# Moving a chunk's reciprocal ahead of the running sums, and work over the seam between two stages, in a fused attention and expert kernel

## The chip, the cores and the metric

The kernel runs on one core of a Trainium2 chip, in one launch. The metric is the device time of a launch in microseconds (us), the median of several runs. A core has five engines that run side by side, each with its own order of instructions: PE (TensorE, the matrix products; PEld are its weight loads), DVE (VectorE), ACT (ScalarE), POOL (GpSimd) and SP (SyncE, which here only issues DMAs). Matrix products write to PSUM, a memory of eight banks; a bank that is to be written again must first have been read by whoever needs its content. All times below are in us.

## The reference

The input `query` has 2048 tokens of 512 values. The output is the sum of the input, an attention and a layer of experts, both of the normalised input:

```python
x = L0_attn_query
xn = _layernorm(x, axis=-1)
x = x + attention(xn, Wq, Wk, Wv, Wout, ...) + experts(xn, gate_w, w1, w3, w2, sw1, sw3, sw2)
```

The attention has 16 heads, each with two causal softmaxes over the same values of width 32 (queries and keys are turned by rotary angles first). The two results are filtered along the sequence and subtracted, then each head is scaled to a root mean square of one and all heads go through Wout:

```python
f1 = jnp.fft.rfft(attn1, axis=1)
f2 = jnp.fft.rfft(attn2, axis=1)
attn_freq = (f1 - lambda_full * f2) * filt[None, :, None, None]
attn = jnp.fft.irfft(attn_freq, n=tgt_len, axis=1)
attn = attn * jax.lax.rsqrt(jnp.mean(attn * attn, axis=-1, keepdims=True) + EPS) * rms_weight
attn = attn * (1.0 - LAMBDA_INIT)
return attn.reshape(bsz, tgt_len, H * 2 * D) @ Wout
```

The experts are eight networks of hidden width 352, of which each token takes the two that a gate scores highest, and one shared network of hidden width 704 that every token takes. Each is `silu(x @ w1) * (x @ w3) @ w2`.

## The kernel before

**The stages.** From 0 to about 100 us the kernel loads the input, normalises and transposes it, makes the values and scores the gate, and sorts the tokens by expert. To about 253 it projects queries and keys, with the rotary turn, and does a part of the shared expert. From 253 to about 1252 runs `middle`: the attention's softmaxes with the experts threaded in. From there `ending` does the filter, the scaling by head, Wout and the final sums.

**The attention's order.** `middle` walks over 8 groups of two heads and, in each, over 4 chunks of 512 queries, from the last chunk to the first (`turns`). A chunk is cut into units, each with the keys of one or a few blocks; masked units, those on the diagonal, come last in a chunk. All units of all chunks stand in one list, `stream`, and the loop takes four of them per step. A step issues, in this order: the scores of two units (ps_s, L764, followed by ACT's exponentials to tiles pt, L777), the products of the previous step's pt with the values (ps_o, L804), the row sums of a chunk that has just ended (`sums`, ps_sum, L830), the scores of two more units, the rest of the products, on POOL the `put` of a chunk that was finished a step ago (L859), and then the part that the change touches:

- `added(before)` adds pt tiles to the running sums on DVE (L821; the first tile of a chunk is copied, L818). They were held back a step, because the sums' tiles were still in use.
- `added(...)` for the unmasked ones of the first two units of this step.
- `finish` (L837) of a chunk that ended a step ago: PE turns the chunk's output and row sums (ps_ot, four transposes, L842, and ps_st, one, L843); DVE takes the reciprocal of the row sums (rcp, L845), scales half of it (L848) and multiplies (o_n, L850).
- `work()` (L954), which takes the next piece of the experts' work, with `added` for the later units between the pieces, until the pace is met.
- `added` for the masked units, and on POOL a step or two of `folded` (L864; lines L870 to L912), the first part of the filter, for a group whose four chunks are through.

Each engine runs its own instructions in this order; nothing is reordered at run time.

**The experts' pieces.** `experts()` (L591) is a generator: each `next` issues a piece and gives back its estimated time. After the shared expert come 36 tiles of routed tokens. One tile takes an `up_first` (xh, L168, with ACT's tanh and DVE's L176), an `up_third` (xg, L168, with DVE's L182), a piece with the transposes of the next tile's tokens (ps_x, L159, and ACT's copy xT, L161) and the product of the tile before (`turned_back`, ps_u, L191, with DVE's copies uT, L193 and L194, and `down`, xy, L201, with ACT's result y_sb, stored by SP). The up weights come in wu, the down weights in wd, both fetched by SP two tiles ahead. The loop takes pieces until `worked / work_all` reaches the share of units done, with four units of lead (L999). `work_all` (L923) comes to 467.6 of the estimates' units.

**The banks.** In `middle` the scores take four PSUM banks, the values' product ps_o one, and a pool of three (fps, L577) serves everything else in turn: ps_sum, ps_ot, ps_st, and every tile of the experts (xh, xg, xy, ps_x, ps_u, wh, wy). A tile that is asked for while all three are held waits until the oldest has been read.

**The end of the attention.** After the loop, the last two chunks are closed one after the other (L1019 on): `sums`, `next(ex)`, `finish`, and `put`, here on DVE. Then the rest of the experts' pieces is issued, and the folds that are left, the last group's on DVE.

**The end stage.** `ending` (L1032) first asks for its tables on ACT's queue (conv, then the shared expert's last down weights, then wo_sb, the weights of Wout) and for the first twelve residual tiles (res: the input by SP's queue, then three sums into it by POOL's). The filter is a set of small products (ps_r and ps_z, L1082) with sums between them on DVE (L1127 on). It gives 16 tiles of 128 tokens, taken as eight `Pair`s: `prepared` makes y on DVE and squares it on ACT, `means` reduces and takes the root on ACT (L1162 on), `scales` refines the root and makes a (L1175) on DVE. A tile then goes `across` (L1198: ps_tr, four transposes on PE, and ACT's copy to aT, L1204), is `projected` (L1207: po, four products with wo_sb, L1210) and `finished` (L1213: DVE adds po to res, L1215, and SP's queue writes it out, L1216). `finished` also issues the loads of the four last res tiles.

Of the kernel before, what the change touches and what calls it, by code (L numbers as in the profile page):

```python
# [8 lines left out]
F32 = mybir.dt.float32  # L9
# [10 lines left out]
P = 128  # L20
T = 2048
E = 512
D = 16
NT = T // P
NE = E // P
# [37 lines left out]
def block_kernel(  # L63
# [7 lines left out]
    nc = tc.nc  # L71
# [206 lines left out]
    with ExitStack() as pools:  # L278
# [95 lines left out]
        for c in range(NE):  # L374
            for i in range(NQC):
                nc.tensor.matmul(
                    gt_ps[32 * i : 32 * i + 32, 0, :], gw_sb[:, c, :], xnT[:, c, i * QC : (i + 1) * QC],
                    start=(c == 0), stop=(c == NE - 1), skip_group_check=True,
# [41 lines left out]
        for t in range(NT):  # L420
# [5 lines left out]
                start=False, stop=(t == NT - 1), skip_group_check=True,  # L426
# [131 lines left out]
    def middle(general):  # L558


        with ExitStack() as pools:
# [358 lines left out]
            for n, turn in enumerate(turns):  # L920
                chunk = Chunk(*turn)
                stream += [(n, chunk, unit) for unit in chunk.units()]
            work_all = (NT - 1 - EARLY) * ((2 * SCH - 1) * 3.45 / TQ + 5.2) + NR * 8.5  # L923
            ex = experts()
            for c in range(NQC):
                load_keys(0, c)
# [43 lines left out]
            for i in range(0, len(stream), 4):  # L970
                units = stream[i : i + 4]
                found = burst(units[:2])
                n, ended = values()
                for c in closing:
                    c.sums()
                    summed += 1
                if n < 2 and not closing:

                    work()
                found += burst(units[2:])  # L980
                while todo:
                    ended += values()[1]
                todo += found
                for c in closed:
                    c.put(nc.gpsimd)
                    if c.qc == 0:
                        ready.append(c.g)
                closed, closing = closing, ended
                held, before = [], held
                added(before)  # L990
                added(u for u in units[:2] if not masked(u))
                later = [u for u in units[2:] if not masked(u)]
                for c in closed:
                    c.finish()
                while True:
                    work()
                    added(later[:1])
                    later = later[1:]
                    if worked / work_all >= (i + 4) / len(stream):  # L999
                        break  # L1000
                added(later)
                added(u for u in units if masked(u))
                if any(map(masked, units)) or not shared:
                    steps = 0
                else:
                    steps = 1 if len(ready) < 2 or any(map(masked, stream[i + 4 : i + 8])) else 2
                for _ in range(steps):
                    if folding is None and ready:
                        folding = folded(ready.pop(0), nc.gpsimd)
                    if folding is not None and next(folding, 0) == 0:  # L1010
                        folding = None
# [20 lines left out]
    def ending():  # L1032
# [3 lines left out]
        with tc.tile_pool(name="tail1", bufs=1) as t1, tc.tile_pool(name="tail", bufs=2) as tp, tc.tile_pool(  # L1036
# [161 lines left out]
            def across(k):  # L1198

                ptr = fps.tile([P, NE, P], F32, tag="f", name="ps_tr")  # L1200
                for c in range(NE):
                    nc.tensor.transpose(ptr[:, c, :], pairs[k // 2].a[:, k % 2, c * P : (c + 1) * P], ident)
                aT = tp.tile([P, NE, P], F32, tag="aT", name="aT")
                nc.scalar.copy(aT, ptr)  # L1204
                return aT

            def projected(aT):  # L1207
                po = fps.tile([P, E], F32, tag="f", name="po")
                for c in range(NE):
                    nc.tensor.matmul(po, aT[:, c, :], wo_sb[:, c, :], start=(c == 0), stop=(c == NE - 1))  # L1210
                return po

            def finished(k, po):  # L1213
                res = came[k]
                nc.vector.tensor_add(res, res, po)  # L1215
                nc.sync.dma_start(out_t[:, order[k], :], res)  # L1216
                for step in range(4):
                    if 12 <= k + 9 - step < NT:
                        fetched(k + 9 - step, step)
# [11 lines left out]
            pairs.append(prepared(1))  # L1231
            pairs[0].means()
            y = result(us, 0)
            nc.vector.tensor_sub(dv, z, dv)
            pairs[0].scales()
            aT = across(0)
            pairs[1].means()
            po = None
            for n in range(NT // 2):
                after = across(2 * n + 1)  # L1240
                ahead, po = po, projected(aT)
                if n + 1 < NT // 2:
                    pairs[n + 1].scales()
                if n == 0:
                    stored(y, ysh[NT - 1], 0.5)
                if n + 2 < NT // 2:
                    pairs.append(prepared(n + 2))
                if n + 1 < NT // 2:
                    aT = across(2 * n + 2)
                if ahead is not None:  # L1250
                    finished(2 * n - 1, ahead)
                if n + 2 < NT // 2:
                    pairs[n + 2].means()
                now, po = po, projected(after)
                finished(2 * n, now)
            finished(NT - 1, po)

    with tc.If(nc.values_load(more[0:1, 0:1], min_val=0, max_val=1) > 0):  # L1258

# [129 lines left out]
```

## Time and profile before

| | us |
|---|---|
| three runs | 1369.66, 1371.17, 1373.96 |
| median | 1371.17 |
| the profiled execution | 1372.31 |
| its span in the trace | 1370.5 |

The mean granted clock of TensorE was 0.992 of full speed. The costliest groups of instructions, weight loads left out (busy us in total, and mean ns of one):

| line and operation | count | busy us | mean ns |
|---|---|---|---|
| L821 DVE, running sums | 576 | 622.1 | 1130 |
| L777 ACT, exponentials | 544 | 527.8 | 1024 |
| L804 PE, product with the values | 2560 | 266.0 | 534 |
| L764 PE, scores | 1280 | 205.4 | 407 |
| L782 POOL, causal mask | 256 | 170.2 | 689 |
| L231 PE, shared expert, up | 352 | 151.2 | 578 |
| L520 PE, queries and keys | 256 | 110.5 | 593 |
| L201 PE, routed experts, down | 216 | 99.8 | 598 |
| L168 PE, routed experts, up (xh) | 288 | 96.9 | 482 |
| L168 PE, routed experts, up (xg) | 288 | 94.1 | 470 |

The prediction shows lines of several views. The **page** gives each engine's busy time and share, and the share of each engine in the **chain**, which is the work that ended last, followed back from the end. The **waits** list, for one engine, which instruction waited for what: total us, number of times, longest. The **timeline** gives instructions in order: start, duration, engine, line, operation, what it writes and reads, shape, count, and in square brackets the idle time before it with what ended it. The **stretches** give, for a window of time, the busy time of each engine in it, the granted clock of TensorE (1.00 is full), the share of the DMA engines' time and GB/s.

### The profile page before, as it was taken

How to read it: one execution, taken by the hardware profiler on the slowest of the kernel's cores; microseconds unless marked ns; L12 is line 12 of the kernel's file. 1: busy time of each engine (PE TensorE's matmuls, PEld its weight loads, DVE VectorE, ACT ScalarE, POOL GpSimd, SP SyncE). 2: the span in 40 equal slices, each digit the busy share in tenths (PEclk: the TensorE clock that was granted, in tenths of full speed). 3: DMA queues.
4: the chain of work that ended last, by engine and by line, in shares of the span. 5: the costliest groups of instructions: out<-in, count | busy, mean ns of one | idle time of the engine just before them, and what ended most of it. 6: DMA issues, size and time to landing. Idle time of an engine off the chain costs nothing.

```text
span 1370.5 us, 20621 instructions
## 1 busy us (share of the span) xinstructions
PE 1325.6 (97%) x7472; PEld 614.9 (45%) x7472; DVE 1005.0 (73%) x1337; ACT 690.6 (50%) x853; POOL 565.9 (41%) x673
## 2 busy tenths in 40 slices
PE   7999999999999999998999999999999999998998
PEld 3444444333443454444444444544444454444543
DVE  7048882378777867867787788798788878787785
ACT  2311110265655656665666566666666656662321
POOL 0001222111401232136964655576468437534863
PEclk9999999999999999999999999999999999999999
DMA  9405662201211122355655656656656565548996
GB/s 376 171 16 181 202 198 80 87 10 37 77 40 32 44 73 67 89 151 173 207 172 167 182 189 195 200 182 193 201 155 215 184 197 187 180 142 261 177 200 142
DMA packets 74689, 206.58 MB, mean 151 GB/s; under 512 B 12028, under 2 KB 12192, under 8 KB 69200
## 3 DMA queue, kind: packets, MB, share of 16 engines
q1 hardware_dynamic: 61840, 177.62, 40.4%
q0 software_dynamic: 11216, 23.31, 8.2%
q10 hardware_dynamic: 1520, 4.23, 0.9%
q8 instruction: 62, 1.02, 0.3%
q14 instruction: 51, 0.42, 0.1%
HBM read 161.26 MB, written 43.85 MB: 150 GB/s over the span
## 4 chain that ended last, share of the span: by engine, by line
PE 68%; DVE 8%; issue 2%; ACT 1%; DMA 1%; POOL 1%; DVEq 0%; ACTq 0%
PE ps_o L804 16%; PE ps_s L764 12%; PE wh L231 9%; PE xh L168 7%; PE xg L168 6%; PE xy L201 6%; PE wy L269 4%; DVE sum L821 3%; PE ps_sum L830 2%; PE po L1210 1%; DMA wd<-in_wex_dram 1%; PE ps_ot L842 1%; PE ps_u L191 1%; PE ps_z L1082 1%; PE ps_x L159 1%
## 5 line engine op out<-in xcount | busy, mean ns | idle before, releaser
L821 DVE TENSOR_TENSOR sum<-sum,pt 128x1024 f32<-128x1024 f32 (+2 forms) x576 | 622.1, 1130 | 32.2 <-ACT pt L777 16.2
L777 ACT ACTIVATE pt<-ps_s 128x1024 f32<-128x1024 f32 x544 | 527.8, 1024 | 177.3 <-PE ps_s L764 110.4
L782 POOL TENSOR_SCALAR_AFFINE_SELECT pt<-pt 128x256 f32<-128x256 f32 x256 | 170.2, 689 | 331.5 <-ACT pt L777 276.0
L804 PE MATMUL ps_o<-pt,vd 128*32 128x512 f32 (+3 forms) x2560 | 266.0, 534 | 1.3 <-POOL pt L782 1.3
L764 PE MATMUL ps_s<-qS,kS 64*128 64x512 f32 (+3 forms) x1280 | 205.4, 407 | 2.0 <-DVEq L1258 1.6
L764 PEld LDWEIGHTS ps_s<-qS,kS 64*128 64x128 f32 x1280 | 97.2, 185 | 173.3 <-issue 95.1
L231 PE MATMUL wh<-xnT,wu 128*128 128x512 f32 (+1 forms) x352 | 151.2, 578 | 0.0
L804 PEld LDWEIGHTS ps_o<-pt,vd 128*32 128x32 f32 x2560 | 66.7, 109 | 130.3 <-issue 116.0
L473 POOL DMA_INDIRECT who<-pairs,slot x32 | 34.2, 1069 | 202.5 <-DVE pairs L470 101.3
L859 POOL TENSOR_TENSOR vd<-o_n 128x128 f32<-128x128 f32 x60 | 43.3, 742 | 172.4 <-DVE o_n L850 149.9
L520 PE MATMUL ps_x<-xnT,wqk_sb 128*128 128x512 f32 x256 | 110.5, 593 | 0.0
L201 PE MATMUL xy<-wd,uT 128*128 128x512 f32 (+1 forms) x216 | 99.8, 598 | 6.5 <-DVE rcp L845 5.0
L168 PE MATMUL xh<-wu,xT 128*128 128x352 f32 x288 | 96.9, 482 | 8.8 <-DVE rcp L845 7.9
L231 PEld LDWEIGHTS wh<-xnT,wu 128*128 128x128 f32 x352 | 64.9, 191 | 72.2 <-issue 58.0
L168 PE MATMUL xg<-wu,xT 128*128 128x352 f32 x288 | 94.1, 470 | 0.0
L520 PEld LDWEIGHTS ps_x<-xnT,wqk_sb 128*128 128x128 f32 x256 | 48.4, 190 | 60.6 <-issue 60.6
L269 PE MATMUL wy<-wd,ws 128*128 128x512 f32 x160 | 74.7, 603 | 0.0
L168 PEld LDWEIGHTS xh<-wu,xT 128*128 128x128 f32 x288 | 54.0, 198 | 36.3 <-DVE rcp L845 9.9
L176 DVE SCALAR_TENSOR_TENSOR xtanh<-xtanh,xh 128x352 f32<-128x352 f32 x36 | 18.7, 520 | 67.2 <-ACT xtanh L175 67.2
L168 PEld LDWEIGHTS xg<-wu,xT 128*128 128x128 f32 x288 | 52.4, 191 | 34.1 <-issue 9.5
L537 ACT CAST hi<-turned 128x1024 fp32r<-128x1024 f32 x16 | 16.7, 1045 | 93.8 <-DVE turned L535 71.5
L242 DVE SCALAR_TENSOR_TENSOR ws<-ws,wh 128x512 f32<-128x512 f32 (+4 forms) x26 | 16.8, 645 | 61.8 <-ACT ws L241 61.7
(239 smaller groups left out, 1413.6 us busy)
## 6 DMA issues: line engine op xcount, KB each, us to landing
wu<-in_wex_dram SPq DMA_DIRECT2D x40, 1408.0 KB
wd<-in_wex_dram SPq DMA_DIRECT2D x39, 768.0 KB
kS<-parts_k SPq DMA_DIRECT2D x128, 128.0 KB
qS<-parts_q SPq DMA_DIRECT2D x256, 64.0 KB
ys<-y_sb SPq DMA_DIRECT2D x36, 256.0 KB
parts_q<-hi SPq DMA_DIRECT2D x32, 256.0 KB
parts_k<-hi SPq DMA_DIRECT2D x16, 256.0 KB
parts_k<-turned SPq DMA_DIRECT2D x16, 256.0 KB
```

Of the source, the lines that this page charges most:

```text
L168: nc.tensor.matmul(dst, xT[:, c, :], w[:, o : o + FI], start=(c == 0), stop=(c == NE - 1))
L201: nc.tensor.matmul(y, uT[:m, ic, :], w[:m, ic * E : (ic + 1) * E], start=(n == 0 and ic == 0), stop=(n == len(pairs) - 1 and ic == NF - 1),)
L231: nc.tensor.matmul(dst, w_sb[o // WUP][0][:, o % WUP : o % WUP + P], x[:, c, :], start=(c == 0), stop=(c == NE - 1))
L269: nc.tensor.matmul(y, us[i][:, t * P : (t + 1) * P], w_sb[i // NF][1][:, i % NF * E : (i % NF + 1) * E], start=(i == 0), stop=(i == SCH - 1),)
L473: nc.gpsimd.indirect_dma_start(out=who, out_offset=bass.IndirectOffsetOnAxis(ap=slot[:, k, t : t + 1], axis=0), in_=pairs[:, k, t, :], in_ ...
L520: nc.tensor.matmul(ps[:, i, :], wqk_sb[st, qk][:, i, c, :], xnT[:, c, cols], start=(c == 0), stop=(c == NE - 1),)
L764: nc.tensor.matmul(to, k, queries[2 * g + h, qc][r, off : off + w], start=True, stop=not general)
L777: nc.scalar.activation(pt[:, :, used], ps[:, :, used], AF.Exp, scale=SCALE)
L782: nc.gpsimd.affine_select(out=part, in_=part, pattern=[[0, 2], [1, P]], compare_op=ALU.is_ge, fill=0.0, base=0, channel_multiplier=-1,)
L804: nc.tensor.matmul(self.o[r : r + 32, off:], vd[:, kb, v0 : v0 + 32], pt[:, s, :], start=first, stop=self.ended, skip_group_check=True,)
L821: nc.vector.tensor_add(to, to, pt)
L859: eng.tensor_add(vd[:, self.qc * TQ : (self.qc + 1) * TQ, v0 : v0 + 32], self.o_n[:, :, h, 0, :], self.o_n[:, :, h, 1, :],)
```

## The change

It has four parts.

1. In the step, `finish` of the chunk that ended a step ago is issued ahead of `added(before)` and of the sums of this step's first two units.
2. The pace is measured against `work_all - left`, with `left = 11.0`. The loop so takes 2.35% less of the estimated work per step, and the generator's last pieces are issued by `next(ex)` between the two last chunks' sums and finishes, and behind them.
3. In the end stage, the first pair's `scales` stands ahead of the subtraction into dv, and in the loop the next `across` stands ahead of the next but one pair's `prepared`. The loads that `finished` issued are a function of their own, `still`, called after it.
4. The last tile's projection is done in two halves of 256 columns, each with its own bank, sum and output transfer, the first on ACT's queue and the second on SP's (`last`).

```diff
--- before.py
+++ after.py
@@ -921,6 +921,7 @@
                 chunk = Chunk(*turn)
                 stream += [(n, chunk, unit) for unit in chunk.units()]
             work_all = (NT - 1 - EARLY) * ((2 * SCH - 1) * 3.45 / TQ + 5.2) + NR * 8.5
+            left = 11.0
             ex = experts()
             for c in range(NQC):
                 load_keys(0, c)
@@ -986,17 +987,17 @@
                     if c.qc == 0:
                         ready.append(c.g)
                 closed, closing = closing, ended
+                for c in closed:
+                    c.finish()
                 held, before = [], held
                 added(before)
                 added(u for u in units[:2] if not masked(u))
                 later = [u for u in units[2:] if not masked(u)]
-                for c in closed:
-                    c.finish()
                 while True:
                     work()
                     added(later[:1])
                     later = later[1:]
-                    if worked / work_all >= (i + 4) / len(stream):
+                    if worked / (work_all - left) >= (i + 4) / len(stream):
                         break
                 added(later)
                 added(u for u in units if masked(u))
@@ -1214,6 +1215,20 @@
                 res = came[k]
                 nc.vector.tensor_add(res, res, po)
                 nc.sync.dma_start(out_t[:, order[k], :], res)
+
+            def last(k, aT):
+
+                for i, eng in enumerate((nc.scalar, nc.sync)):
+                    half = slice(i * E // 2, (i + 1) * E // 2)
+                    po = fps.tile([P, E // 2], F32, tag="f", name="po")
+                    for c in range(NE):
+                        nc.tensor.matmul(po, aT[:, c, :], wo_sb[:, c, half], start=(c == 0), stop=(c == NE - 1))
+                    res = came[k][:, half]
+                    nc.vector.tensor_add(res, res, po)
+                    eng.dma_start(out_t[:, order[k], half], res)
+
+            def still(k):
+
                 for step in range(4):
                     if 12 <= k + 9 - step < NT:
                         fetched(k + 9 - step, step)
@@ -1231,8 +1246,8 @@
             pairs.append(prepared(1))
             pairs[0].means()
             y = result(us, 0)
+            pairs[0].scales()
             nc.vector.tensor_sub(dv, z, dv)
-            pairs[0].scales()
             aT = across(0)
             pairs[1].means()
             po = None
@@ -1243,17 +1258,21 @@
                     pairs[n + 1].scales()
                 if n == 0:
                     stored(y, ysh[NT - 1], 0.5)
+                if n + 1 < NT // 2:
+                    aT = across(2 * n + 2)
                 if n + 2 < NT // 2:
                     pairs.append(prepared(n + 2))
-                if n + 1 < NT // 2:
-                    aT = across(2 * n + 2)
                 if ahead is not None:
                     finished(2 * n - 1, ahead)
+                    still(2 * n - 1)
                 if n + 2 < NT // 2:
                     pairs[n + 2].means()
-                now, po = po, projected(after)
-                finished(2 * n, now)
-            finished(NT - 1, po)
+                if n + 1 < NT // 2:
+                    now, po = po, projected(after)
+                    finished(2 * n, now)
+                    still(2 * n)
+            finished(NT - 2, po)
+            last(NT - 1, after)
 
     with tc.If(nc.values_load(more[0:1, 0:1], min_val=0, max_val=1) > 0):
 
```

## The prediction

> **What bounds the kernel now.** I read the page's busy shares and chain first.
>
> ```profile
> span 1370.5 us, 20621 instructions
> PE 1325.6 (97%) x7472; PEld 614.9 (45%) x7472; DVE 1005.0 (73%) x1337; ACT 690.6 (50%) x853; POOL 565.9 (41%) x673
> PE 68%; DVE 8%; issue 2%; ACT 1%; DMA 1%; POOL 1%; DVEq 0%; ACTq 0%
> ```
>
> TensorE is busy 97% of the span and leads the chain. The change adds no PE work but eight short matmuls, so it can win only what PE idles (45 us, much of it before 100 us) and what PE loses at half clock. Next, therefore, PE's waits:
>
> ```profile
> PE xh L168 <- DVE rcp L845: 7.9, 2, 4.6
> ...
> PE ps_r L1082 <- issue: 5.2, 1, 5.2
> PE xy L201 <- DVE rcp L845: 5.0, 3, 2.2
> PE ps_tr L1202 <- DVE a L1175: 2.6, 4, 1.6
> ...
> PE po L1210 <- ACT aT L1204: 1.2, 2, 1.0
> ```
>
> Columns: total us, times, longest. Five waits are for the reciprocal of `finish`: ps_ot and ps_st hold two of three fps banks, and an experts' tile needs one back, which comes free when rcp has read ps_st. The timeline of PE places them and the one before ps_r (start, us, idle before):
>
> ```profile
> 630.34 5.06 PE L168 MATMUL xh<-wu,xT 128*128 128x352 f32 x8 [4.64 <-DVE rcp L845]
> ...
> 759.63 5.06 PE L168 MATMUL xh<-wu,xT 128*128 128x352 f32 x8 [3.30 <-DVE rcp L845]
> ...
> 861.56 2.85 PE L201 MATMUL xy<-wd,uT 128*128 128x512 f32 x6 [1.13 <-DVE rcp L845]
> ...
> 1005.08 2.84 PE L201 MATMUL xy<-wd,uT 128*128 128x512 f32 x6 [2.18 <-DVE rcp L845]
> ...
> 1128.55 2.84 PE L201 MATMUL xy<-wd,uT 128*128 128x512 f32 x6 [1.72 <-DVE rcp L845]
> ...
> 1256.99 3.58 PE L1082 MATMUL ps_r<-vd,conv 128*128 128x512 f32 x4 [5.24 <-issue]
> ```
>
> The waits sum to 12.97 in attention and 5.24 at the start of the end stage. The two xh tiles took 5.06; in the chain, xh of the same shape takes 2.37. The stretches say why (first the stretch and its length, then PE, PEld, DVE, ACT, POOL busy, clock, DMA share, GB/s):
>
> ```profile
> 626.00:630.00 4.00, 0.00 (x0) 0.00 (x0) 4.00 (x5) 0.50 (x1) 3.49 (x4) 0.85 1.00 325
> 630.00:632.00 2.00, 1.66 (x3) 1.17 (x4) 1.73 (x6) 0.00 (x0) 0.65 (x2) 0.50 0.87 201
> ...
> 634.00:636.00 2.00, 2.00 (x5) 1.20 (x4) 0.07 (x1) 0.46 (x1) 0.87 (x2) 0.59 0.23 80
> ```
>
> After the 4.64 the granted clock was 0.50 for about 5 us, so the wait costs about 2.7 (5.06 less 2.37) more. It was 0.50 after the 3.30 and before ps_r too, and 0.84 or more around the 2.18 and 1.72. What held the reciprocal, on VectorE:
>
> ```profile
> 623.44 4.95 DVE L821 TENSOR_TENSOR sum<-sum,pt 128x256 f32<-128x256 f32 x3
> 628.32 1.80 DVE L818 COPY sum<-pt 128x1024 f32<-128x1024 f32 x2
> 630.04 0.25 DVE L845 RECIPROCAL rcp<-ps_st 128x16 f32<-128x16 f32 x1
> ```
>
> Two copies stand directly ahead, but the adds before them are slow: the first 256-wide add took 2.69 beside POOL's fold (L875 at 623.32, L876 at 624.57, 1.3 each); elsewhere that shape takes 0.43. The change moves the copies, not these masked adds.
>
> **Part A, attention (finish ahead, pace 456.6 instead of 467.6).** The sums go against the profiled run's 1372.31 (span 1370.5 and 1.8 around it). Two adds or copies (1.2 to 2.3 by rows) go behind the reciprocal; the previous step's six masked adds stay ahead. The lower pace also shifts which experts' tile follows ps_st, which decides when the third bank is wanted. By the instruction order of the changed kernel, with these rows' durations:
> - at 630: the next tile becomes ps_x, then xy. The finish at 1128 has that pattern: adds end at 1127.04, the bank is wanted at 1126.83, so without copies the wait is about 0.5. The fold still runs beside the adds and adds about 3.5: 4.0 remain, and the half clock's 2.7. Bounds 0 (another phase to POOL) and 4.64.
> - at 759: only xg follows ps_st, the bank is wanted 4.1 later: 0, and the 2.7 goes. At 861, two adds of 1.15 go behind: 0. At 1005: 0. At 1128: 0.1.
> - at 884, no wait now: ps_u and xh come without an xg in front: 0.55 new.
>
> Left: 4.0 + 0 + 0 + 0 + 0.1 + 0.55 = 4.65, so −8.3, and −2.7 of clock. Where the routed experts begin (605), xT's copy falls behind two exps: 1.2 where PE waits 0.74 now: +0.5. A = **−10.5**. The copies moved are hidden as long as DVE has time behind o_n: there its L176 waits 1.57 to 4.1 for ACT in rows after finishes.
>
> On the clock, the Trainium skill, "TensorE: Matmul & The Clock Gate", section "What's actually happening", says that half clock follows an idle window of about 3.4 us. The rows of 4.64 and 5.24 agree; 3.30 is under that figure and cost 2.7 all the same, and a wait of 1.59 at 255 was followed by 0.73 to 0.84. By the rule alone the 3.30 would cost its own length only, and the sum would be 2.7 smaller.
>
> **Part B, into the end stage.** By the order, PE issues ps_u, xh, xg, xy, ps_u and xy behind the last ps_s, where it now issues ps_u and one xy. The surplus, xh 2.37, xg 2.5, xy 2.84 and ps_u 0.48, is 8.2 that PE no longer does before that ps_s. Now ps_r starts 18.2 after that ps_s ends (1238.77 to 1256.99), of which waits are 5.24 and 0.52. Without waits 12.46; with the 8.2 and new waits of 0.45 (uT's copies behind ps_u, and a bank) 21.1. Against now: 21.1 − 18.2 − 8.2 = −5.3. ps_r itself keeps full clock (3.58 to about 1.9), but DVE then sets the pace: its fold and ws rows run 9.6 us from 1253.60, and L1128, which frees ps_r's bank, ends at 1263.8. So the next product gains only 0.85 of the 1.7. B = **−6.15**. Bounds: 0 if PE waits for the fold as long as now behind the added work, −5.3 − 1.7 = −7.0 if DVE keeps up. Queues: the loads of wd and wo_sb on ACT's queue now stand behind the last y_sb, conv still ahead of it; wo_sb is wanted near 1270, some 10 us of cover; if that is gone, each us late is a us.
>
> **Part C, order in the end stage.** DVE's chain: sub (1.21 by L1131's shape) covered ACT's root; without it in front, scales waits for the root: the first a is 0.7 earlier, the later ones 0.3 later. ps_tr waits for a four times: +0.3. aT ahead of the squares on ACT takes away po's 0.96, but the transposes after it then wait for a: 0 net (bounds −1.0 and +1.0). C = **+0.3**.
>
> **Part D, last tile by halves.** The rows now: last matmul ends 1364.36, then
>
> ```profile
> 1364.40 0.69 DVE L1215 TENSOR_TENSOR res<-res,po 128x512 f32<-128x512 f32 x1 [2.75 <-PE po L1210]
> ```
>
> and the transfer, whose traffic lies in 1365 to 1367, and silence to 1370.5. The second half's add is 0.42 (a 128x256 row): −0.27. 128 KB instead of 256: between 0 and −0.9, I take −0.35. Sixteen half-wide passes for eight: same columns, between 0 and +0.5 for issue; 0. D = **−0.6**. The Trainium skill, "DMA: Bandwidth & Descriptors", section "Anatomy of one DMA — SWDGE (gpsimd) path", speaks against halving: about 2.0 us fixed, plus bytes at 436 GB/s; 128 KB less saves 0.3 by it. The tail of silence agrees with a large fixed part.
>
> Sum: −10.5 − 6.15 + 0.3 − 0.6 = −16.95, 1355.4 for a run like the profiled one. That run is 1.14 above the median of the runs (1371.17), so the forecast is **1354.2**.
>
> **The rivals.**
> - *Clean*: all five waits go, the first too (the fold falls elsewhere). 4.0 + 2.7 more: 1347.5. For it: copies and adds on DVE shift by the pace. Against: the masked adds stay ahead. Chance 0.15.
> - *Leftover*: DVE is late by the masked adds beside folds, not by the copies; the waits shrink by 1.3 each (−6.5), no clock returns, B brings half (−3): about 1361.5. For it: 4.95 against 1.80 in the rows. Chance 0.22.
> - *No gain*: the waits move to other finishes, and PE's wait before ps_r is the fold's and stays behind the added tiles: 1368 to 1372. Against: five of about 30 finishes wait now, by pattern. Chance 0.06.
> - *Slower*: DVE parks at the reciprocal. At a dozen finishes it already waits 0.7 to 0.8 for ps_st; now two adds wait behind it, up to 3.5 later, and behind them xtanh and the prob buffers that the next exps need. Slack is L176's 1.57 to 4.1. It decides from 0.8 lost on PE at each of 27 unstalled finishes (21.6, against −16.95 and the 4.1 of the measurement); at 0.9 it is 24.3, about 1378.5. Against: DVE has 27% idle, and PE waited 1.3 in all for pt. Chance 0.09.
>
> **How the numbers follow.** Main case 0.48 (1350 to 1360: the bounds of the first wait, B and C), clean 0.15, leftover 0.22, none 0.06, slower 0.09. The likeliest gives 1354.2. From 1345 to 1365 holds main, clean and leftover, 0.85, less some of each one's tails: 0.8. A measurement of this kernel tells about 0.3% (4.1 us) from no change: faster is below 1367.1. Main, clean, leftover: 0.85, less 0.01 of leftover's tail; same 0.07 (none and that tail); slower 0.09.
>
> **What would show it.** PE's waits for rcp: about 5 in total instead of 12.9, one long one near 625 with 0.50 after it. At 759, xh of 2.4 instead of 5.06. The wait before ps_r gone, two xy and an xg behind the last ps_s. PE busy down about 4. The last add 0.42. Wrong, if PE waits for pt or for ACT's copies grow by more than 3, if rcp is waited for as long as now, or if folds rather than copies hold most finishes.

## The result, and the profile after

| | before | changed |
|---|---|---|
| median us | 1371.96 (14 runs) | 1370.14 (14 runs) |
| lowest and highest | 1369.66, 1376.21 | 1364.83, 1376.51 |
| ratio, 95% interval | | 0.9988, 0.997 to 1.0006 |
| profiled execution, its span | 1372.31, 1370.5 | 1370.38, 1368.2 |

No change that the measurement can tell, where 1354.2 was forecast with a range of 1345 to 1365. The page of the changed kernel:

```profile
span 1368.2 us, 20621 instructions
PE 1324.3 (97%) x7480; PEld 615.1 (45%) x7480; DVE 1015.4 (74%) x1338; ACT 690.9 (50%) x853; POOL 613.7 (45%) x673
PE 72%; DMA 12%; DVE 8%; POOL 4%; ACT 2%; issue 2%; ACTq 0%; DVEq 0%; POOLq 0%
```

PE does the same work in 2.3 us less span. What strikes is POOL: the same 673 instructions, 613.7 us instead of 565.9. The waits of PE in the changed kernel (total, times, longest):

```profile
...
PE xy L201 <- DVE rcp L845: 6.5, 2, 4.2
PE ps_o L804 <- POOL pt L782: 5.4, 4, 3.1
PE ps_tr L1203 <- DVE a L1176: 4.1, 5, 1.9
PE ps_z L1083 <- DVE vd L1129: 3.3, 1, 3.3
PE ps_s L764 <- ACT pt L777: 2.5, 2, 2.0
...
PE xh L168 <- DMA wu<-in_wex_dram: 1.8, 1, 1.8
```

The 12.9 for the reciprocal became 6.5, and the 5.2 before ps_r is gone. In their place stand waits for pt, which POOL masks (1.3 before, 5.4 now), 3.3 in front of a ps_z, and smaller ones. The timeline of PE places the long ones:

```profile
630.37 4.33 PE L201 MATMUL xy<-wd,uT 128*128 128x512 f32 x6 [4.17 <-DVE rcp L845]
...
679.18 1.41 PE L804 MATMUL ps_o<-pt,vd 128*32 128x512 f32 x8 [3.11 <-POOL pt L782]
...
766.59 4.49 PE L201 MATMUL xy<-wd,uT 128*128 128x512 f32 x6 [2.33 <-DVE rcp L845]
...
1260.53 15.67 PE L1083 MATMUL ps_z<-xnT,conv 128*128 128x512 f32 x32 [3.33 <-DVE vd L1129]
```

The waits at 759, 861, 1005 and 1128 are gone, as forecast; that at 630 stayed, as forecast; that at 766 is new. Both xy rows are long (2.84 at full clock).

A table by stage says how much each forecast missed. Attention is from the first ps_s to the end of the last; seam from there to the end of the filter's products (the start of the 56 wh behind them); end from there to the span's end. All from the timelines of PE.

| us | start | attention | seam | end |
|---|---|---|---|---|
| before | 255.05 | 983.72 | 46.77 | 84.92 |
| changed | 253.88 | 978.01 | 51.95 | 84.36 |
| difference | −1.2 | −5.7 | +5.2 | −0.6 |
| forecast | 0 | −18.7 | +2.05 | −0.3 |

8.2 us of experts' work moved from attention to seam, so the forecast for attention is A less that, −10.5 − 8.2, and for the seam B plus it, −6.15 + 8.2. Net of the moved work, attention got 2.5 longer, not 10.5 shorter; the seam won 3.0 instead of 6.15. The 8.2 is the sum of the pieces' rows in the forecast; in the traces the stretch from the last ps_s to ps_r, waits left out, grew by 7.5 (12.46 to 20.0). With 7.5 in place of 8.2, attention got 1.8 longer and the seam won 2.3; the sum is the same.

VectorE shows the trade in one view. Its waits between 230 and 1245, before the change:

```profile
DVE xtanh L176 <- ACT xtanh L175: 67.2, 33, 4.1
...
DVE uT L193 <- PE ps_u L191: 16.5, 9, 3.9
...
DVE rcp L845 <- PE ps_st L843: 9.1, 12, 0.8
```

and after it:

```profile
DVE rcp L845 <- PE ps_st L843: 57.0, 26, 4.8
...
DVE xtanh L176 <- ACT xtanh L175: 41.4, 24, 2.5
...
DVE uT L193 <- PE ps_u L191: 7.3, 8, 2.9
```

VectorE now stands at the reciprocal for 48 us more; 35 of them it used to stand elsewhere, so standing there is cheap. The adds behind it, however, now run more often beside `put` on POOL, as counted further down.

### The profile page after: what moved, and what is told of

Same layout as the page of the kernel before. It is cut to its first block, busy times and chain, and to the rows that moved or that the text cites. A ratio compares the mean times of both kernels' runs of the same rounds, so it can differ in the third digit from the quotient of the medians.

```text
span 1368.2 us, 20621 instructions
## 1 busy us (share of the span) xinstructions
PE 1324.3 (97%) x7480; PEld 615.1 (45%) x7480; DVE 1015.4 (74%) x1338; ACT 690.9 (50%) x853; POOL 613.7 (45%) x673
## 4 chain that ended last, share of the span: by engine, by line
PE 72%; DMA 12%; DVE 8%; POOL 4%; ACT 2%; issue 2%; ACTq 0%; DVEq 0%; POOLq 0%
PE ps_o L804 16%; PE ps_s L764 12%; DMA who<-pairs,slot 10%; PE wh L231 8%; PE xy L201 6%; PE xh L168 6%; PE xg L168 6%; PE wy L269 4%; PE ps_tv L364 4%; PE ps_sum L830 2%; DMA wu<-in_wex_dram 1%; PE ps_ot L842 1%; POOL pt L782 1%; PE ps_x L159 1%; PE ps_u L191 1%
## 5 line engine op out<-in xcount | busy, mean ns | idle before, releaser
L821 DVE TENSOR_TENSOR sum<-sum,pt 128x1024 f32<-128x1024 f32 (+2 forms) x576 | 628.3, 1142 | 14.9 <-POOL pt L782 6.8
L782 POOL TENSOR_SCALAR_AFFINE_SELECT pt<-pt 128x256 f32<-128x256 f32 x256 | 176.6, 719 | 282.4 <-ACT pt L777 236.7
L804 PE MATMUL ps_o<-pt,vd 128*32 128x512 f32 (+3 forms) x2560 | 268.5, 534 | 5.6 <-POOL pt L782 5.4
L859 POOL TENSOR_TENSOR vd<-o_n 128x128 f32<-128x128 f32 x60 | 64.3, 1091 | 153.6 <-DVE o_n L850 153.6
L804 PEld LDWEIGHTS ps_o<-pt,vd 128*32 128x32 f32 x2560 | 67.1, 109 | 136.4 <-issue 115.0
L201 PE MATMUL xy<-wd,uT 128*128 128x512 f32 (+1 forms) x216 | 102.6, 612 | 6.5 <-DVE rcp L845 6.5
L168 PE MATMUL xh<-wu,xT 128*128 128x352 f32 x288 | 92.2, 463 | 3.2 <-DMA wu<-in_wex_dram 1.8
L1067 POOL DMA_INDIRECT res<-ys,slot x32 | 53.8, 1683 | 22.6 <-DMA res<-ysh 10.5
L364 PE MATMUL ps_tv<-wv_sb,xnT 128*128 128x512 f32 x128 | 58.9, 613 | 0.7 <-ACT xnT L361 0.7
```

Of the source, the lines that this page charges most:

```text
L168: nc.tensor.matmul(dst, xT[:, c, :], w[:, o : o + FI], start=(c == 0), stop=(c == NE - 1))
L201: nc.tensor.matmul(y, uT[:m, ic, :], w[:m, ic * E : (ic + 1) * E], start=(n == 0 and ic == 0), stop=(n == len(pairs) - 1 and ic == NF - 1),)
L364: nc.tensor.matmul(pv, xnT[:, c, t * P : (t + 1) * P], wv_sb[:, c, :], start=(c == 0), stop=(c == NE - 1))
L782: nc.gpsimd.affine_select(out=part, in_=part, pattern=[[0, 2], [1, P]], compare_op=ALU.is_ge, fill=0.0, base=0, channel_multiplier=-1,)
L804: nc.tensor.matmul(self.o[r : r + 32, off:], vd[:, kb, v0 : v0 + 32], pt[:, s, :], start=first, stop=self.ended, skip_group_check=True,)
L821: nc.vector.tensor_add(to, to, pt)
```

## The experiments

The theory after the result: (1) the finish ahead does win, as forecast by its mechanism; (2) the lower pace, taken from every step, shifts all the experts' tiles, and so chooses anew which of them meet a finish, POOL's masks or a weight load; (3) the seam is held by something that the last tile's store does; (4) the end stage's order is worth nothing. The rival: what is left for the end costs attention as much as it gives, or VectorE's waiting at the reciprocal does. "Ratio" is to runs of the kernel before on the same chip.

### The finish alone

```diff
+                for c in closed:
+                    c.finish()
                 held, before = [], held
                 added(before)
                 added(u for u in units[:2] if not masked(u))
                 later = [u for u in units[2:] if not masked(u)]
-                for c in closed:
-                    c.finish()
```

> The kernel before with the finish alone moved ahead of the two adds; pace and end stage as before. Theory A (the move trades one wait for another): VectorE's wait at the reciprocal for ps_st grows from 9 us to about 50, PE's waits for the reciprocal fall from 13 us to 5 to 8, PE's waits for pt and for the experts' inputs grow by about as much, and the time is within 3 us of before. Rival B (the prediction's part A is right and the other parts lose it): PE's waits for the reciprocal fall by 8 us, nothing else grows, and the time is 6 to 10 us under before.

Measured: 1366.87 against 1370.91, ratio 0.9967 (0.9954 to 0.9979). Attention 976.98, 6.7 less than before. VectorE waited 66.8 at the reciprocal, PE's waits for it fell from 12.9 to 5.4, and those for pt rose from 1.3 to 3.9:

```profile
PE xh L168 <- DVE rcp L845: 3.9, 2, 2.9
PE ps_o L804 <- POOL pt L782: 3.9, 4, 1.6
...
PE xy L201 <- DVE rcp L845: 1.5, 2, 1.0
```

The seam, where nothing was changed, is 1.7 longer: the clock was at half for 6.8 us in it, for 3.4 before. So A's trade exists but is not even: the move alone gains about 4.5 us by the times. The half clock at 759 went too (xh 2.63 instead of 5.06). Parking at the reciprocal, the mechanism of the forecast's slower rival, happens and does not decide.

### The lower pace alone

```diff
+            left = 11.0
...
-                    if worked / work_all >= (i + 4) / len(stream):
+                    if worked / (work_all - left) >= (i + 4) / len(stream):
```

> The kernel before with the pace of 456.6 alone, so that the same pieces are left for the attention's end; finish behind the adds. Theory A (the seam gives only part of the forecast, since the last tile's store holds the end stage's first ACT instruction): the last ps_s ends 7 to 9 us earlier, ps_r starts about 5 earlier, the products after it only 2 to 3 earlier; time 1 to 4 us under before. Rival B (the prediction's part B): products after ps_r 6 us earlier, time 6 under before.

Measured: 1370.89 against 1370.91, ratio 1.0 (0.9992 to 1.0009). Attention 977.36, which is 1.8 more than before once the 8.2 that moved are counted; waits for the reciprocal of 5.35 at 626 and 4.24 at 764, and four shorter ones. The last ps_s ended 7.5 earlier, ps_r started 5.7 earlier, the products after it ended 1.6 earlier; 1.1 of each of these is a shorter start in this execution. The seam, net of the 8.2, gains 2.3 of the forecast 6.15, and attention takes 1.8 of that back.

### The end stage alone, and its order alone

The first kernel is the kernel before with the change's parts 3 and 4, the second with part 3, of which this is the core:

```diff
-            nc.vector.tensor_sub(dv, z, dv)
             pairs[0].scales()
+            nc.vector.tensor_sub(dv, z, dv)
...
+                if n + 1 < NT // 2:
+                    aT = across(2 * n + 2)
                 if n + 2 < NT // 2:
                     pairs.append(prepared(n + 2))
-                if n + 1 < NT // 2:
-                    aT = across(2 * n + 2)
```

> The kernel before with the end stage's order and the last tile by halves alone. By the prediction's parts C and D: -0.3 us, from +1 to -1.5. Attention and seam as before, the last add 0.42, the span after the last product 0.6 shorter. A rival in which the order costs: the waits of ps_tr for a grow by over 1 and the time is the same or up to 1 us longer.

> The kernel before with the end stage's order alone (scales ahead of the subtraction, across ahead of prepared). By the prediction's part C +0.3 with bounds of 1 either way. By the trace of the run with the end stage's order and halves, the stretch from the first ps_tr to the last product is over 1 us longer: if that is the order's, it shows here too and the time is 0.5 to 1 us over before; if it is the halves', that stretch is as before within 0.3.

Measured: 1371.47 against 1370.91, ratio 1.0005 (0.9996 to 1.0014), and for the order alone 1372.0 against 1370.84, ratio 1.001 (1.0001 to 1.0019). The stretch from the first ps_tr to the last product is 67.0 in both against 65.6 before, while the first ps_tr comes 0.7 earlier: the order costs 0.65 to 0.75 in these two traces, and 0.35 to 0.9 in the six others that have it. What the aT copy no longer waits for, the transposes wait for a. The first row is the kernel before, the second the order alone:

```profile
1313.05 0.66 PE L1202 MATMUL ps_tr<-cst,a 128*128 128x128 f32 x4 [0.30 <-DVE a L1175]
```

```profile
1313.25 0.66 PE L1202 MATMUL ps_tr<-cst,a 128*128 128x128 f32 x4 [1.86 <-DVE a L1175]
```

Both start at a time that VectorE sets. The halves do what was worked out: in the changed kernel the 16 half-wide passes take 3.62 where eight took 3.60, the last add takes

```profile
1363.06 0.42 DVE L1227 TENSOR_TENSOR res<-res,po 128x256 f32<-128x256 f32 x1 [1.30 <-PE po L1225]
```

and from its start to the span's end it is 5.15 instead of 6.06.

### A tile of its own for the last store

On ACT's timeline in the changed kernel, the first tanh of the end stage stands still for 6.4 us:

```profile
1250.79 0.69 ACT L210 ACTIVATE y_sb<-xy,wcol 128x512 f32<-128x512 f32 x1 [5.05 <-PE xy L201]
1250.87 0.33 ACTq L144 DMA_DIRECT2D wd<-in_wex_dram  x1
1251.25 0.45 ACTq L1049 DMA_DIRECT2D wo_sb<-in_wout_dram  x1
1257.89 0.38 ACT L241 ACTIVATE ws<-wh 128x256 f32<-128x256 f32 x1 [6.41 <-DMA ys<-y_sb]
1258.17 0.58 ACT L1126 COPY first<-ps_r 128x512 f32<-128x512 f32 x1
```

The last y_sb is written at 1250.79 and its store issued at 1251.51. The tile ws of the end stage is laid on memory that y_sb had, so it may not be written until the store has landed, and two big loads were issued just ahead of that store (whether they slowed it was not tested). `first`, which has had its data since ps_r, waits behind ws on ACT, and L1128 on VectorE behind both. Before the change this store left 8 us earlier, at 1243.36, and L241 did not meet it:

```profile
1253.72 0.39 ACT L241 ACTIVATE ws<-wh 128x256 f32<-128x256 f32 x1 [3.65 <-DVE vd L859]
```

```diff
                 rp = pools.enter_context(tc.tile_pool(name="routed", bufs=2))
+                y_last = pool("last", 1).tile([P, E], F32, name="y_last")
...
-                down(*late)
+                down(*late, into=y_last)
```

> The changed kernel, where the last routed tile's y_sb has a tile of its own that no tile of the end stage lies on. Theory A (in the changed kernel ACT's first tanh of the end stage, L241, waits for the store of that y_sb to land, and the copy first, the sums at L1128 and the second product queue behind it): L241 runs about 5 us earlier, PE's 3.3 us wait before the second product goes to below 1, and the time is 2 to 3 us under the changed kernel. Rival B (VectorE's fold sets it): the wait before the second product stays above 2.5 and the time is that of the changed kernel.

Measured: 1367.42 against 1370.91, ratio 0.9977 (0.9963 to 0.999). ACT in this kernel:

```profile
1251.90 0.38 ACT L241 ACTIVATE ws<-wh 128x256 f32<-128x256 f32 x1 [0.85 <-PE wh L231]
1253.48 0.59 ACT L1127 COPY first<-ps_r 128x512 f32<-128x512 f32 x1 [1.19 <-PE ps_r L1084]
```

L241 runs 6.0 earlier. The seam is 48.89 instead of 51.95, so net of the moved 8.2 it gains 6.1, as forecast (6.15). The wait before the product fell from 3.33 to 1.97 only, not below 1: PE still waits for VectorE there, which the rival named. Of the 3.06 that the seam gained over the changed kernel, this is 1.36; the other 1.70 is clock, since the 32 products behind the wait, 15.67 in the changed kernel, took 13.97 here, at full clock. That part is luck: in the best version below the same wait of 1.97 was followed by half clock. By the times the gain over the changed kernel is about 1.5 (ratios of 0.9988 and 0.9977, to different runs of before), and the intervals overlap; the trace is the evidence.

### No folds on POOL

```diff
-                        folding = folded(ready.pop(0), nc.gpsimd)
+                        ready.pop(0)
+                        folding = iter(())
...
-            for each in ([folding] if folding else []) + [folded(g, nc.gpsimd) for g in ready]:
+            for each in []:
```

> The changed kernel with POOL's folds left out (the first part of the filter for seven of eight groups is not computed, so PE, ACT and VectorE do the same work and POOL does less). Theory A (the folds slow VectorE's masked adds beside them and hold POOL's masks): PE's wait for the reciprocal at 630 falls from 4.17 to below 1.5, PE's waits for pt from 5.4 to below 1, the half clock behind them goes, and the time is 8 to 14 us under the changed kernel. Rival B (six masked adds are late by their number alone): the wait at 630 stays over 3 and the time falls by less than 4.

Measured: 1356.2 against 1370.84, ratio 0.9891 (0.9876 to 0.9905). VectorE ahead of the finish near 630 in the changed kernel:

```profile
622.43 7.71 DVE L821 TENSOR_TENSOR sum<-sum,pt 128x768 f32<-128x768 f32 x6
630.07 0.25 DVE L845 RECIPROCAL rcp<-ps_st 128x16 f32<-128x16 f32 x1
```

and with POOL's folds left out:

```profile
620.59 4.08 DVE L821 TENSOR_TENSOR sum<-sum,pt 128x768 f32<-128x768 f32 x6
624.58 0.25 DVE L845 RECIPROCAL rcp<-ps_st 128x16 f32<-128x16 f32 x1
```

The same six adds take 3.6 less, PE's wait there falls from 4.17 to 0.53, and PE's waits for pt in all from 5.4 to 0.45. Attention is 13.0 shorter than in the changed kernel, though PE waits 3.7 for weights there (1.8 in the changed kernel). So the folds delay both: VectorE's adds run slow beside them, and POOL's masks stand behind them. This kernel leaves out a part of the filter, so its time measures the folds and is not a gain to be had.

### The same work left, but taken from the last quarter

```diff
-                    if worked / (work_all - left) >= (i + 4) / len(stream):
+                    part = (i + 4) / len(stream)
+                    if worked >= work_all * part - left * max(0.0, 4 * part - 3):
                         break
```

> The changed kernel with the full pace up to three quarters of the attention and the 11.0 taken off over the last quarter; the pieces left at the end are the same. Theory A (which experts' tile meets which finish decides): PE's wait at 766 goes, that at 630 is about 2.9 instead of 4.2, and the time is 4 to 7 us under the changed kernel. Rival B (leaving work costs PE in attention as much as it gives later): time within 2 of the changed kernel.

Measured: 1360.87 against 1370.84, ratio 0.9927 (0.9914 to 0.994), about 8 under the changed kernel with the same pieces left, a little more than theory A's 4 to 7. Its waits near the places of before:

```profile
626.42 4.33 PE L168 MATMUL xh<-wu,xT 128*128 128x352 f32 x8 [2.81 <-DVE rcp L845]
...
676.25 1.41 PE L804 MATMUL ps_o<-pt,vd 128*32 128x512 f32 x8 [1.57 <-POOL pt L782]
...
758.76 2.63 PE L168 MATMUL xh<-wu,xT 128*128 128x352 f32 x8 [0.96 <-DVE rcp L845]
```

The wait at 766 is gone, that at 679 is half, and PE waits for no weight load. Attention with the 8.2 counted is 977.6, as with the finish alone (977.0). The best version below has the same order in attention and comes to 978.2; the changed kernel and the run with the store's own tile, both with the even pace, come to 986.2 and 984.4. So leaving this work did not cost attention; taking it evenly from every step did, by 6 to 9 us.

### Other amounts, taken evenly

The changed kernel with one number changed, here the first of two:

```diff
-            left = 11.0
+            left = 20.0
```

The second has 5.5.

> The changed kernel with left = 20.0 instead of 11.0. By the instruction order, the tile behind ps_st is now xg at the finishes that lie near 630 and 766, where it is ps_x and xy in the changed kernel. Theory A (which tile meets which finish decides): PE's waits of 4.17 and 2.33 there and the half clock behind them go, PE waits for the reciprocal under 3 us in all, and the time is 3 to 8 us under the changed kernel, though twice as much is left. Rival B (what is left costs attention in proportion): the time is that of the changed kernel or up to 5 over it.

> The changed kernel with left = 5.5. By the instruction order, ps_u and xh follow ps_st near 630 (a wait of 2.8 to 2.9 in two runs that had them there), ps_x and xy near 759, ps_u and xh near 766. Theory A: waits for the reciprocal at all three places, 5 to 9 us in all, some half clock, less left for the seam: time within 3 us of the changed kernel. Rival B (cost in proportion to what is left): attention 4 us better than with 11.0, waits for the reciprocal below 4, time 2 to 5 under the changed kernel.

Measured: 1370.84 against 1371.27, ratio 0.999 (0.9979 to 1.0002), and 1371.62, ratio 1.0005 (0.9989 to 1.0022). With 20.0 the order of the tiles said that the waits for the reciprocal go, and they did (1.1 in all), yet the time did not fall: theory A was right on the wait and wrong on the time. PE's waits in that kernel:

```profile
PE ps_o L804 <- POOL pt L782: 8.5, 5, 5.3
...
PE xh L168 <- DMA wu<-in_wex_dram: 2.9, 1, 2.9
...
PE xy L201 <- DVE rcp L845: 1.1, 2, 0.6
```

With 5.5, waits of 2.67 and 2.78 at the reciprocal, 4.9 for pt, 6.1 for the weights. From the first ps_s to the end of the filter's products it took 1030.5 before, 1030.0 with 11.0, 1030.7 with 20.0, 1033.2 with 5.5, and 1022.8 with 11.0 from the last quarter. Neither theory's line holds: the cost is not in proportion to what is left, and it is not at the finishes alone. An even shift moves PE's waits among the finishes, POOL's masks and the weight loads. Which amount is best can't be read from one execution of each: the next section has one with 20.0 whose attention is 3.5 shorter in the same order.

### The two versions that put the parts together

The first is the changed kernel with the diffs of the last store's own tile and of the last quarter, and the order of the end stage undone. The second is the same without the last quarter's diff and with

```diff
-            left = 11.0
+            left = 20.0
```

> Finish ahead, the full pace up to three quarters of the attention and the 11.0 taken off over the last quarter, the last y_sb in a tile of its own, the end stage in the order of before, last tile by halves. Theory A (the uniform pace moved which experts' tile meets which finish and so took back the finish's gain; the store held the seam): attention 6 us shorter as in the run with the finish alone, seam 6 shorter, tail 0.5 shorter, time 9 to 13 under before. Rival B (whatever the pace, what is left for the seam costs in attention what it gains there): 3 to 6 under before.

> left = 20.0 at the uniform pace, with the last y_sb in a tile of its own and the end stage in the order of before (last tile by halves, finish ahead). Theory A: 2 to 4 us under the run that has left = 20.0 alone, so 8 to 15 under before; VectorE's fold is done before PE is through with what is left, so PE's wait before the second product goes to 0. Rival B (leaving more costs attention): as the run with left = 20.0, less 2.5, at or above 1366.

Measured: 1358.39 against 1370.84, ratio 0.9907 (0.9893 to 0.9921), and 1364.67 against 1371.27, ratio 0.9948 (0.9931 to 0.9966). The first beats both kernels, by 12.7 and by 11.1 us. In its trace attention, net of the 8.2, is 5.5 shorter than before, the seam 4.4 and the end 0.8, where theory A had 6, 6 and 0.5. In the second, the wait before the second product fell to 0.49 (of an expected 0), and its waits for pt were 7.8. It is 6.2 under the run that has 20.0 alone, where 2 to 4 were expected. Attention is 966.7 in its trace and 970.2 in that of the run with 20.0 alone, with the same order of instructions and the same idle time of PE (15.6 and 15.7), but with half clock for 6.8 us in the first and for 17.1 in the second. Traces of one order in attention differ by 0.7 to 3.5 us there, so the splits by stage in this document hold to about that.

## Why the prediction was wrong, point by point

**Part A, the copies behind the reciprocal.** The mechanism was right: the finish alone took 7.5 of 12.9 us of waits away and 4.5 us (2.9 to 6.3) of time. The list by finishes held where it was made: 4.0 forecast at 630 and 4.17 measured, nothing at 759, 861, 1005 and 1128; the new 0.55 at 884 did not come. The 3.5 of slow adds there measured 3.6 in the run without folds.

**The step that failed** is the list of five finishes as the whole account of attention: the lower pace came into it only as the new neighbours of those five, and the moved copies only as "hidden as long as DVE has time behind o_n". Attention was 13.0 worse than forecast, and the runs split that. The finish alone made it 6.7 shorter, not 10.5: 3.8 short, with 2.6 more of waits for pt, which POOL masks and which the forecast, following VectorE and PE, left out. The pace cost the most: with the same finish and the same pieces left, attention is 8.7 longer in the changed kernel than with the work taken from the last quarter (6.2 in the pair that also has the store's own tile).

In the changed kernel, idle of PE is 9.7 of the 13.0 (it rose by 1.85, forecast −7.8) and slower busy time 3.3 (0.6 more than the moved work explains, forecast −2.7). The idle by the waits: pt 5.4 for 1.3 (+4.2); a new wait of 2.33 at 766, less small errors (+1.9 for the reciprocal in all); the first chunk's exps (+2.5); a weight load (+1.3). The first chunk's 2.5 is not in the run with the store's own tile, which has the same order there, and the weight load's wait is 0.3 in it; by that run, attention net of the moved work is 0.7 longer, not 2.5. Of the busy time, 0.4 is clock: the xy at 630 and at 766 took 4.33 and 4.49, 3.1 above two at full clock, where 2.7 was forecast to stay. Most of the rest stands in the products with the values (L804, 266.0 busy before and 268.5 after); the eight behind the wait at 679 took 1.41, where eight without a wait take 1.06.

Beside the fold, the move itself slowed POOL. `put` in the kernel before and in the changed one (count, busy us, mean ns of one; then its waits):

```profile
L859 POOL TENSOR_TENSOR vd<-o_n 128x128 f32<-128x128 f32 x60 | 43.3, 742 | 172.4 <-DVE o_n L850 149.9 <-PE ps_s L764 22.5
```

```profile
L859 POOL TENSOR_TENSOR vd<-o_n 128x128 f32<-128x128 f32 x60 | 64.3, 1091 | 153.6 <-DVE o_n L850 153.6
```

A `put` that had one of VectorE's sums (L821, L818) beside it for over 0.3 of its time took 1.14 us on average, any other 0.45; of the 60, 25 had one before and 56 in the changed kernel. The folds are not the cause: without them the mean of `put` is still 1090 ns. All runs with the finish ahead and folds in place have POOL 45 to 70 us busier in all, and that with the pace alone does not (564.4). The Trainium skill, "SBUF — State Buffer", section "Who interferes with whom", states that VectorE instructions with two SBUF inputs, and copies in a two-port mode, contend with GpSimd for one pair of ports, and that in such a mode the one that comes second blocks for the whole instruction. The rows agree in kind: adds and copies now follow o_n, and `put`, which o_n also releases, runs beside them. They do not show the ports.

**Part B, the seam.** The step that failed is the account of queues, which looked at what ACT's loads wait behind and at wo_sb's cover, but not at the memory on which the end stage's first tiles lie, and who still reads it. It cost 3.1: 1.4 of wait and 1.7 of the half clock behind it. With the last y_sb in its own tile the seam gave 6.1 of the forecast 6.15, but that is in part luck: ps_r came 20.0 after the last ps_s, not 21.1, from there to the end of the filter's products it took 28.9, not 27.7, and the half clock stayed away. In the best version, with the same tile, it came, and the seam gave 4.4.

**Part C** was forecast at +0.3 and came to 0.65 to 0.75 in the two traces made for it, and +1.4 (0.1 to 2.6) in time: small, and the sign right. **Part D** was forecast at −0.6; in the changed kernel the tail behind the last product is 0.9 shorter, in the other runs with halves 0.3 to 0.95, and in one without them 0.4, so a part of it is chance; the halves are as fast on PE. The fit in the Trainium skill, "DMA: Bandwidth & Descriptors", section "Anatomy of one DMA — SWDGE (gpsimd) path", which the prediction sets against halving, is given there for transfers that GpSimd issues; these are issued by ACT and SP.

**Sum.** Forecast −16.95 for the profiled run, measured −2.3: attention 13.0 short, seam 3.1 short, end 0.3 and the start 1.2 better. Of the rivals, "no gain" (0.06) came in, with its place right (waits move to other finishes, and a wait of the seam stays behind the added tiles) and its reason for the seam in part: of the 3.33 there, 1.36 was the store's, and the 1.97 left is VectorE's.

Open: which of POOL's delays each wait for pt follows was not separated, and the waits for weight loads under an even pace were not traced to one cause.

## What to carry to other kernels

When work is moved in a schedule that a pace threads together, the whole weave shifts: cost the move by all the meeting points, or move it so that the weave stays (here, from the last quarter). Work carried over a seam of memory pools brings its last store with it; look up what the next stage's first tiles are laid on. And an engine that is moved off the path still competes: what now runs beside VectorE's adds is part of the price.

## What was not expected of the hardware

Waits of PE between 2.1 and 3 us went either way: after 2.33 an xy took 4.49, after 2.81 an xh took 4.33, but after 2.67 an xh took 2.63 and after 2.18 an xy 2.84. The Trainium skill, "TensorE: Matmul & The Clock Gate", section "What's actually happening", has a free-running window of about 3.4 us. The clock records of the traces agree with such a window: within each of the thirteen, every change of the granted clock lies on one grid of 3.41 us, half clock lasts one to three steps of it, and the grid lies elsewhere against the work in each execution.

They do not agree with a window that must be wholly idle. From 250 us on, all 41 steps of the grids in which PE was idle for over 0.55 of the step were followed by half clock; of the steps at full clock with less than 0.45, none was; between the two it went either way. So in these runs the length of a wait decides less than how much of it falls into one step. The 1.97 before the second product shows it, first in the run with the store's own tile, then in the best version (the columns as in the prediction):

```profile
1257.17:1260.58 3.41, 1.79 (x5) 0.87 (x5) 3.31 (x5) 0.00 (x0) 1.85 (x2) 1.00 1.06 407
1260.58:1263.99 3.41, 3.41 (x9) 1.52 (x8) 0.52 (x1) 1.01 (x1) 1.78 (x3) 1.00 1.08 321
```

```profile
1248.71:1252.13 3.42, 1.46 (x4) 0.49 (x3) 2.76 (x6) 0.00 (x0) 1.01 (x1) 0.99 1.06 410
1252.13:1255.54 3.41, 3.41 (x5) 1.35 (x4) 1.93 (x2) 0.00 (x0) 2.05 (x3) 0.50 1.08 320
```

PE was busy for 1.79 of the step in the one, and the next step ran at full clock; in the other for 1.46, and the next ran at half. In the changed kernel, the 3.11 before 679 fell half into each of two steps (0.50 idle in both) and cost no clock, while the 2.33 before 766 lay in one (0.66) and did. What a wait costs beyond its own length is therefore in part chance, the prediction's 2.7 included.
